# Block order, operand layout and output steps of a relative-attention kernel changed on one core

## The chip, the core and the metric

The kernel runs on one core of a Trainium2 chip. The core has TensorE (PE in the profile; PEld is its weight load), VectorE (DVE), ScalarE (ACT), GpSimd (POOL) and SyncE (SP), which here issues every transfer, and 16 DMA engines. Each engine works through its own instructions in order. The metric is the device time of one execution in microseconds (us), the median of several runs.

## What is computed

A transformer block over x of 16 sequences, 512 positions, 128 features: layer norm, then attention with relative positions (16 heads of 8 features) plus a feed-forward network (FFN) with weights of +1 and -1, plus the residual.

```python
q = (xn @ Wq + bq).reshape(B, S, H, dh)          # k, v alike; B=16, S=512, H=16, dh=8
p = (pe @ Wp).reshape(S, H, dh)
content = einsum('bihd,bjhd->bhij', q + u_bias, k)
pos = _relative_shift(einsum('bihd,jhd->bhij', q + v_bias, p))
attn = softmax((content + pos) * scale, axis=-1)
head = einsum('bhij,bjhd->bihd', attn, v).reshape(B, S, D)
out = x + head @ Wo + bo + ffn(layernorm(x))      # three layers, 256-512-512-128, relu between
```

`_relative_shift` pads one column and reshapes, so that the position score of a row comes from a window that slides with the row, and beyond the diagonal from the next row.

## The kernel before, in words

**Setup** (functions from `norm` to `more`). x is loaded by sequence (`load_x`, four buffers, XB), normalized on VectorE (`norm`, L318 to L339), transposed on TensorE (L509) and split into a high and a low half of 16 bits (`split`). FFN layers run block by block, one sequence a block (`ffn_layer`, L640, four banks of PSUM, F_BANKS; `ffn_last`, L674); ScalarE writes the high half of each result (L617), VectorE the low one (L618). The result and the residual (`ffn_residual`, added on POOL at L662) go to `res_scr` in DRAM (L691). Between these, a queue of steps of the attention's preparation is worked off at a rate set by SPAN, so that it is empty after 12.3 of 15 blocks: `project_q`, `project_k`, `project_v` per sequence, `positions` and `windows`. A projection is scaled and biased from PSUM into a 32-bit tile on ScalarE (`scaled`, L528), ScalarE casts that to its high half (`halves_to`, L502), and POOL subtracts to get the low half (L503). Content queries of two sequences are kept apart with zeros (`qu_b`, cleared at L492) and written with the zeros to `qu_scr`; keys go to `k_scr`, values in rows of 36 numbers per head to `v_scr`, position queries stay in SBUF (`qv_all`) until `quads_stored` writes them by quarter to `qv_scr`. When the queue is empty, `more` takes one step of `stores` at a time: `quads_stored(0)`, `load_head(0)`, `load_queries(0, 0)`, `quads_stored(1)`, `load_queries(0, 1)`. In setup a planner orders the instructions of each engine; it may take a ready one forward.

**Attention.** Work is cut into units. A unit is four rows of every 128-row chunk of the queries of one head, for all 16 sequences against all keys. A head has NU = 32 units in two half blocks (`up`) of UP = 16, and NL = 4 sets of position and content queries (`q_t`, two buffers, UL = 8 units to a set). Before, the order is head by head: the units of both half blocks of head 0, then head 1. `load_head` brings a head's keys, windows and values in 13 transfers, `load_queries` a set of queries in 12. They are called at the unit steps "A" and all their transfers are issued there on SP. TensorE, VectorE and ScalarE follow an order written out by hand (STEPS, one string per cycle of two units): A and B are the scores of a unit's first and second half (`scores`, L797 content, L813 and L826 position), F, G and H the maxima (L840, L845), T and N the transposes and row maxima (L850, L854), X and Y the subtraction of the maximum (L859) and the exponentials (L869), V the weighted values of the half block before (`weighted`, L887, into `a_t`). A half block of a head is called a pair in the code and takes eight V steps. During the first eight cycles, W steps do the last sequence's FFN instead of V.

**Sums.** After four V steps half the sequences of a pair are complete. `stored_sums` loads the denominators of the copied bank to `den` (L921), stores the sums by four transfers to `sum_scr`, and two V steps later `inverted` takes the reciprocals (L929), stores them (L931), and at the end of a head calls `divided`: load `raw` and `rden`, multiply on POOL (L946), store to `head_scr` (L947), all issued at once. So SP stands at L947 until POOL is done.

**Tail.** `last_steps` loads the sums of heads 0 to 14 for both half blocks (`load_sums`), the residuals (`load_res`) and the last head's denominators (`load_rden`) in the last two pairs. POOL divides the last head's first half (L978). For the last pair, `last_sums` takes the denominators by a product with `sel` (L904), reciprocals (L906) and a multiplication (L907), and `last_moved` copies to the sums. Then `output_of` multiplies all sums of both half blocks with Wo (L986), adds the residual (L994) and stores (L997).

## Time and profile before

| | |
|---|---|
| time, median of 3 runs | 1366.68 us (1365.07 to 1369.44) |
| the profiled execution | 1368.64 us |
| its span, first to last instruction | 1366.9 us, mean granted TensorE clock 0.985 |
| busy: PE, DVE, ACT, POOL | 1289.9, 1113.8, 882.3, 130.7 us |
| DMA | 243607 packets, 160.22 MB, mean 117 GB/s |
| first scores L797 / first weighted values L887 | 263.7 / 309.1 us |
| last exponentials L869 end | 1315.7 us |

The span has three stages, each read from its own rows. The setup lasts to about 264 us; FFN and preparation share the engines. From about 312 to 1312 us the written-out cycle repeats. The rest is the tail. Busy shares of the whole say little about a stage: DVE's 81% is a mean over stages with 46%, 86% and 100%. A PE row's duration contains the pipeline, so the spacing of equal matmuls is its cost: four of L640's 128x512 take 1.03 us together, one alone 0.38.

### The profile page before, as it was taken

What the parts mean: (1) busy time and instruction counts of PE and PEld (TensorE: products, weight loads), DVE (VectorE), ACT (ScalarE), POOL (GpSimd) and SP (SyncE); (2) the same over time, 40 slices, a digit from 0 to 9 for tenths busy, and PEclk for the clock granted to TensorE, in tenths of its full rate; (3) what the DMA queues carried; (4) which work ended last, traced back from release to release, by engine and by line L of the source; (5) the groups of instructions that cost most, each with busy time, mean ns of one, the idle gap of its engine ahead of it and who ended that gap; (6) DMA issues with size and microseconds to landing.
All of it is one profiled execution on the core that took longest, in us unless ns stands there. A gap on an engine that the chain in (4) does not pass through costs nothing. (4 is left out here: it accounts for less than half of the span.)

```text
span 1366.9 us, 55407 instructions
## 1 busy us (share of the span) xinstructions
PE 1289.9 (94%) x23061; PEld 952.7 (70%) x23061; DVE 1113.8 (81%) x2723; ACT 882.3 (65%) x1456; POOL 130.7 (10%) x115
## 2 busy tenths in 40 slices
PE   4988889979999999999999999999999999999966
PEld 2545555667777777777777777777777777777735
DVE  8988754678888888888888888888888888788846
ACT  4576668466666666666666666666666666666630
POOL 4243445010000000000000000000000000000011
PEclk9999999999999999999999999999999999999987
DMA  4597869863243323333333323332333353323288
GB/s 117 168 234 198 202 159 264 245 193 89 76 104 79 98 80 92 81 98 90 84 93 89 94 78 97 82 96 77 96 84 93 87 123 86 99 78 81 69 145 190
DMA packets 243607, 160.22 MB, mean 117 GB/s; under 512 B 79510, under 2 KB 227100, under 8 KB 243356
## 3 DMA queue, kind: packets, MB, share of 16 engines
q1 hardware_dynamic: 243356, 156.69, 43.9%
q8 instruction: 180, 2.95, 0.9%
q14 instruction: 71, 0.58, 0.2%
HBM read 96.34 MB, written 59.48 MB: 114 GB/s over the span
## 5 line engine op out<-in xcount | busy, mean ns | idle before, releaser
L869 ACT ACTIVATE e<-s,e_scale 128x512 f32<-128x512 f32 x1024 | 673.1, 686 | 319.9 <-PE s L859 319.5
L840 DVE TENSOR_REDUCE m<-s 128x256 bf16<-128x512 f32 x512 | 351.0, 686 | 132.0 <-PE s L826 131.9
L845 DVE TENSOR_TENSOR m<-s,m 128x256 bf16<-128x256 f32 x1024 | 428.5, 418 | 18.5 <-PE s L826 0.6
L797 PE MATMUL s<-q,k 128*128 128x64 f16 x8192 | 407.0, 193 | 4.0 <-DMA q<-qu_scr 2.1
L859 PE MATMUL s<-ident_b,nm 128*128 128x256 bf16 x2048 | 353.0, 275 | 2.3 <-DVE nm L854 2.3
L813 PE MATMUL s<-q,win 128*128 128x128 f16 (+1 forms) x4096 | 342.6, 206 | 0.0
L797 PEld LDWEIGHTS <-k 128*128 128x128 f16 x8192 | 334.3, 98 | 11.0 <-DMA q<-qu_scr 2.2
L887 PE MATMUL a_t<-e,v 128*9 128x256 f32 x4032 | 267.0, 382 | 0.7 <-ACT e L869 0.6
L813 PEld LDWEIGHTS <-win 128*128 128x128 f16 x4096 | 232.2, 98 | 0.2
L826 PE MATMUL s<-q,win_d 128*128 128x64 f16 x2048 | 227.7, 193 | 0.8 <-DMA q<-qv_scr 0.6
L859 PEld LDWEIGHTS <-nm 128*128 128x128 bf16 x2048 | 145.1, 98 | 117.2 <-DVE m L845 78.8
L854 DVE TENSOR_REDUCE nm<-t_t 128x2 bf16<-128x256 bf16 x512 | 208.8, 408 | 2.4 <-PE t_t L850 2.4
L887 PEld LDWEIGHTS a_t<-e,v 128*9 128x9 f32 x4032 | 86.5, 90 | 81.8 <-issue 2.5
L850 PE MATMUL t_t<-ident_b,m 128*128 128x128 bf16 x1024 | 141.0, 219 | 1.0 <-DVE m L845 0.9
L826 PEld LDWEIGHTS <-win_d 128*128 128x128 f16 x2048 | 130.2, 98 | 1.2 <-issue 1.1
L946 POOL TENSOR_TENSOR raw<-raw,rden 128x512 f32<-128x512 f32 x15 | 19.1, 1273 | 987.6 <-DMA rden<-rden_scr 762.8
L850 PEld LDWEIGHTS <-m 128*128 128x128 bf16 x1024 | 81.0, 97 | 32.7 <-DVE m L845 1.7
L640 PEld LDWEIGHTS <-e 128*128 128x128 f16 x512 | 49.5, 98 | 62.1 <-issue 14.8
L896 ACT COPY av<-a_t 128x256 f32<-128x256 f32 x126 | 47.0, 373 | 32.3 <-PE a_t L887 17.9
L618 DVE SCALAR_TENSOR_TENSOR h2l<-s,h2h 128x512 f16<-128x512 f32 x45 | 30.9, 686 | 37.0 <-ACT h2h L617 36.8
L640 PE MATMUL s<-h1l,e 128*128 128x512 f16 x180 | 47.1, 379 | 0.5 <-DVE h1l L618 0.4
L617 ACT ACTIVATE h2h<-s 128x512 f16<-128x512 f32 x45 | 26.9, 597 | 32.1 <-PE s L640 32.0
(176 smaller groups left out, 905.3 us busy)
## 6 DMA issues: line engine op xcount, KB each, us to landing
q<-qv_scr SPq DMA_DIRECT2D x512, 64.0 KB
q<-qu_scr SPq DMA_DIRECT2D x256, 64.0 KB
qu_scr<-k SPq DMA_DIRECT2D x32, 256.0 KB
k_scr<-hv SPq DMA_DIRECT2D x64, 128.0 KB
qu_scr<-win SPq DMA_DIRECT2D x32, 256.0 KB
qv_scr<-e SPq DMA_DIRECT2D x16, 512.0 KB
k<-k_scr SPq DMA_DIRECT2D x64, 128.0 KB
win<-p_scr SPq DMA_DIRECT2D x64, 79.5 KB
```

What stands on the lines that cost most here:

```text
L640: nc.tensor.matmul(ph, lhsT=w[:, t, f * P : (f + 1) * P], rhs=h[t][m], start=(m == 0 and t == 0), stop=(m == 1 and t == n - 1),)
L797: nc.tensor.matmul(sp[:, c % 2, :, :, 4 * g : 4 * g + 4].rearrange("p a r (n m) -> p n (a r) m", m=2), lhsT=kt[:, g, c * P : (c + 1) * P], ...
L813: nc.tensor.matmul(blocks[:, x0 : x0 + (NC + 1) * (len(cs) - 1) + 1 : NC + 1], lhsT=win[h % 2][:, side, y0 : y0 + P], rhs=qp[:, side, :, c ...
L826: nc.tensor.matmul(blocks[:, x0 : x0 + NC + 2 : NC + 1, 2 * t : 2 * t + 2], lhsT=win_d[h % 2][:, t, UP_OFF - 4 * u : WIND - 4 * u], rhs=qd ...
L840: nc.vector.tensor_reduce(st["m"], flat(st["ps"][0]).rearrange("p c x -> p x c"), AX.X, ALU.max)
L845: nc.vector.tensor_tensor(st["m"], flat(st["ps"][1])[:, c], st["m"], ALU.max)
L850: nc.tensor.transpose(st["pt"][:, f, :], st["m"][:, f * P : (f + 1) * P], ident_b)
L854: nc.vector.tensor_reduce(st["nm"], st["pt"], AX.X, ALU.max, negate=True)
L859: nc.tensor.matmul(flat(st["ps"][half])[:, :, f * P : (f + 1) * P], lhsT=st["nm"][:, f : f + 1].to_broadcast([P, P]), rhs=ident_b.unsqueez ...
L869: nc.scalar.activation(st["eT"][:, :, cs, :, i0 : i0 + 4].rearrange("p b c a r -> p (c a) b r"), st["ps"][half].rearrange("p c a r b -> p ...
L887: nc.tensor.matmul(bank[32 * r : 32 * r + VW, g], lhsT=v_t[h % 2][:, v0 : v0 + VW], rhs=pair["eT"][:, b, c], start=(c == 0 and (g == 0 or ...
L896: nc.scalar.copy(pair[half][:, g], bank[:, g])
```

## The change

The change does the following.

- **Order.** The pairs run first half block of heads 0 to 15, then the second half block of heads 0 to 15. Only two sets of queries belong to a pair; a head's keys, windows and values are loaded once for each half block. Buffers go by the pair's parity (`m`), not the head's.
- **Loads.** Scratch layouts are turned so that `load_head` is four transfers (of which the windows read overlapping runs), the values one more (`load_values`, now rows of 144 bytes from `v_scr`, stored in long runs), and `load_queries` two for content and eight for position. They are put into a list, `loading`, from which each A step issues two. Content queries come as pairs of sequences without zeros; POOL clears the half that must be zero after each load (`content`).
- **Halves.** The scale is put into the weights; `halves_to` reads the projection in PSUM twice, ScalarE for the high half, VectorE for the low one. q is projected for two sequences at once into two banks of its own. The FFN has three banks instead of four, x six buffers instead of four, SPAN is 13.4. Clearing of q_t moves from `project_k` behind `ffn_residual`; residuals are added two and two.
- **Sums.** `stored_sums` stores the whole bank in one transfer. The steps `inverted`, `inverse_stored`, `divided`, `stored` follow one another at the F steps of four cycles; `divided` works per pair (128x256) and stores straight into `all_sums` in SBUF, or for the second half block of heads 0 to 4 (EARLY) into `early_scr`, loaded later.
- **Output.** The first half block's 16 sequences are multiplied with Wo in pairs 17 to 20, each after an odd V step, in the free half of `a_t` (`first_output`; VectorE's addition, two stores and the loads of a later residual follow at an F step). The second half block's are left for the tail (`last_output`, eight steps of two sequences), where SP and ACT both issue transfers and the last two pairs' denominators are taken by `last_sums`.

```diff
+    def load_head(h, m):
+
+        k = k_scr.rearrange("t (d h) n g j -> n (t d) h (g j)", h=H)[:, :, h]
+        p = p_scr.rearrange("t (d h) s j -> (t d) h (s j)", h=H)[:, h]
+        pd = pd_scr.rearrange("t (d h) s n j -> (t d) h (s n j)", h=H)[:, h]
+        flat_p, flat_d = (t[m].rearrange("p n j -> p (n j)") for t in (win, win_d))
+        side = 2 * (WIND + 1)
+        moves = [
+            (k_t[m].rearrange("p g j -> p (g j)"), k),
+            (flat_p[:, : 2 * WIN + 4], shifted(p, 4, 1, 0, 2 * WIN + 4)),
+        ]
+        for r in range(2):
+            moves.append((flat_d[64 * r : 64 * r + 64, : side - 1], shifted(pd, 2, side, 1 - r, side - 1)))
+        return [lambda a=a: nc.sync.dma_start(*a) for a in moves]
+
+    def load_values(h, m):
+        nc.sync.dma_start(v_t[m].rearrange("p (b f) -> p b f", b=B), v_scr[:, :, h])
+
+    def load_queries(h, l):
+
+        m = l % 2
+        qv = qv_scr.rearrange("t (d h) r l a u b -> (t d) h r l (a u b)", h=H)[:, h, :, l]
+        qu = qu_scr.rearrange("t (d h) q l g i m -> (t d) h q l (g i m)", h=H)[:, h, :, l]
+
+        def content(q):
+            rows = slice(64 * q, 64 * q + 64)
+            nc.sync.dma_start(
+                qc_t[m][rows, q].rearrange("p g i m -> p (g i m)"), shifted(qu[:, q], 2, 0, 0, 8 * P)
+            )
+            for n in (2 * q, 2 * q + 1):
+                nc.gpsimd.memset(qc_t[m][32 * n : 32 * n + 32, q, :, :, 1 - n % 2], 0.0)
...
+        def halves_to(src, n, hi, lo):
+
+            nc.scalar.activation(hi, src, AF.Identity, bias=b_cols[:, n : n + 1])
+            for r in range(4) if len(src.shape) == 4 else [slice(None)]:
+                nc.vector.scalar_tensor_tensor(
+                    lo[:, r], src[:, r], b_cols[:, n : n + 1], hi[:, r], ALU.add, ALU.subtract
+                )
...
         def project_q(b):
+
+            for n in range(2):
+                nc.tensor.matmul(
+                    q_banks[:, n],
+                    lhsT=wq_d,
+                    rhs=x2T[b + n].rearrange("p (a l m) -> p l a m", a=NC, l=NL),
+                    start=True,
+                    stop=True,
+                )
+            qu = qu_b[b // 2 % 2]
+            halves_to(q_banks.rearrange("p n j -> p j n"), 0, *qu)
             for m in range(2):
                 for part in Q_PARTS[m]:
+                    nc.sync.dma_start(
+                        qu_scr[part, :, b // 2 % 2, :, b // 4], qu[m].rearrange("p (l i) n -> p l (i n)", l=NL)
+                    )
+            halves_to(
+                q_banks.rearrange("p n (q r) -> p r q n", r=4), 1, *[q[:, :, :, b : b + 2] for q in qv_all]
+            )
...
+            if 2 <= b < 10:
+                with tc.issue_after(last.ins):
+                    for n in range(2):
+                        clear_queries(2 * (b - 2) + n)
...
-        stores = [lambda: quads_stored(0), lambda: load_head(0), lambda: load_queries(0, 0)]
-        stores += [lambda: quads_stored(1), lambda: load_queries(0, 1)]
+        stores = [[lambda: quads_stored(0)], load_head(0, 0), load_queries(0, 0)]
+        stores += [[lambda: quads_stored(1)], load_queries(0, 1)]
...
+            nc.sync.dma_start(
+                sum_scr[h, :, half].rearrange("w r i -> r w i"), av.rearrange("p g i -> p (g i)")
+            )
             bs = slice(8 * half, 8 * half + 8)
-            for r in range(4):
-                b = 8 * half + 2 * r
-                dst = sum_scr[h, :, b : b + 2, up, :] if h < H - 1 else sums[up][L0:L1, b : b + 2]
-                nc.sync.dma_start(dst, av[32 * r : 32 * r + DH])
 
             def inverted():
                 nc.vector.reciprocal(den, den)
-                inv = rden_scr[h, bs, up]
-                nc.sync.dma_start(inv.rearrange("b (q m) -> b q m", q=16), den)
-                if h == H - 1:
-                    load_rden(half)
-                elif up == 1 and half == 1:
-                    divided(h)
+                return inverse_stored() if n == 2 * H - 2 else inverse_stored
+
+            def inverse_stored():
+                nc.sync.dma_start(rden_scr[h, bs].rearrange("b (q m) -> (b q) m", q=16), den)
+                if half == 1:
+                    return lambda: divided(pair, B)
+                if n == 2 * H - 2:
+                    return lambda: divided(pair, B // 2)
 
             return inverted
 
-        def divided(h):
-
-            raw, rden = (wk.tile([P, S], F32, tag=name, name=f"{name}_{h}", bufs=1) for name in ("raw", "rden"))
-            nc.sync.dma_start(raw, sum_scr[h].rearrange("w b u i -> (w b) (u i)"))
-            nc.sync.dma_start(
-                rden, rden_scr[h].rearrange("b u i -> b (u i)").unsqueeze(0).to_broadcast([DH, B, S])
-            )
+        def divided(pair, nb):
+
+            h, up = pair["h"], pair["up"]
+            raw, rden = (
+                wk.tile([P, 2 * P], F32, tag=name, name=f"{name}_{pair['n']}", bufs=1)[: DH * nb]
+                for name in ("raw", "rden")
+            )
+            nc.sync.dma_start(raw, sum_scr[h].rearrange("w x r (g i) -> w (x r g) i", g=2)[:DH, :nb])
+            nc.sync.dma_start(rden, rden_scr[h, :nb].unsqueeze(0).to_broadcast([DH, nb, 2 * P]))
             nc.gpsimd.tensor_tensor(raw, raw, rden, ALU.mult)
-            nc.sync.dma_start(head_scr[h * DH : (h + 1) * DH].rearrange("w b u i -> w b (u i)"), raw)
+            if up and h < EARLY:
+                dst = early_scr[h * DH : (h + 1) * DH]
+            else:
+                dst = all_sums[rows_of_head(h)]
+
+            def stored():
+                nc.sync.dma_start(dst[:, :nb], raw)
+
+            return stored
...
+        def first_output(b, free):
+
+            products(a_t[:, free], b)
+
+            def added():
+                t = first_res.pop(b)
+                nc.vector.tensor_tensor(t, a_t[:, free], t, ALU.add)
+                res_rows(t, 0, b, store=True)
+                load_first(b + 2)
+
+            return added
...
+        def last_output(b0, step):
+
+            out_banks.append(out_banks.pop(0))
+            po = out_banks[-1].rearrange("p (b i) -> p b i", b=2)
+            bs = slice(b0, b0 + step + 1, step)
+            for x in range(2):
+                products(po[:, x], b0 + step * x)
+            nc.vector.tensor_tensor(last_res[:, bs], po, last_res[:, bs], ALU.add)
+            for b in (b0, b0 + step) if step > 1 else (slice(b0, b0 + 2),):
+                b = b if step == 1 else slice(b, b + 1)
+                for m in range(2):
+                    (nc.sync, nc.scalar)[m].dma_start(
+                        half_rows(out, 1, m, b),
+                        last_res[64 * m : 64 * m + 64, b].rearrange("p b (k d) -> p (b k) d", d=D),
+                    )
...
+        loads = [(h, 2 * up + l) for up in range(2) for h in range(H) for l in range(2)]
...
+                if n % UL == 1 and 2 <= nl < len(loads):
+                    loading += load_queries(*loads[nl])
+                if n % UP == 1 and nl + 1 < len(loads):
+                    loading += load_head(loads[nl + 1][0], (n // UP + 1) % 2)
+                if n % UP == 4:
+                    loading.append(lambda h=h, m=n // UP % 2: load_values(h, m))
+                for _ in range(2):
+                    if loading:
+                        loading.pop(0)()
+                if n % 2 and outputs:
+                    filled.append(first_output(*outputs.pop(0)))
...
+                if n % 2 == 0:
+                    due = [more for more in (do() for do in due) if more]
...
+                if k == 0 and n == H + 1:
+                    load_first(0)
+                    load_first(1)
+                if k % 2 and H < n < H + 5:
+                    outputs.append((4 * (n - H - 1) + k // 2, k // 2 % 2 ^ 1))
+                if k == 1 and n == H + 6:
+                    nc.sync.dma_start(all_sums[: EARLY * DH], early_scr)
+                if n < 2 * H - 2:
+                    if k % 4 == 2 and later:
                         due.append(later.pop(0))
+                    if k % 4 == 3:
+                        later.append(stored_sums(pair, k // 4))
+                elif k in (2, 4):
+                    due.append(later.pop(0))
+                elif k == 3:
+                    later.append(stored_sums(pair, 0))
+                    load_last()
+                elif k == 6:
+                    last_sums(pair, 1, 0)
...
+        pair = pairs[2 * H - 1]
+        moved(pair, 0, (0, 1), [nc.sync, nc.scalar])
+        last_output(0, 1)
+        last_sums(pair, 1, 1)
+        moved(pair, 1, (0,), [nc.sync, nc.scalar])
+        last_output(2, 1)
+        moved(pair, 1, (1,), [nc.sync, nc.scalar])
+        last_output(4, 1)
+        last_output(6, 1)
+        for b in (8, 12, 9, 13):
+            last_output(b, 2)
```

## The prediction

> **What bounds the kernel now.** I read the slices of the page first, then the busy time by stage, then the order of time inside the stages in which TensorE is not full, and last the waits.
>
> ```profile
> PE   4988889979999999999999999999999999999966
> DVE  8988754678888888888888888888888888788846
> DMA  4597869863243323333333323332333353323288
> ```
>
> Three stages can be seen: a setup of eight slices (to 264 us, where the first scores start at L797), a long loop with PE at 9 everywhere, and a tail in the last two slices. The stage view gives the middle of the setup, the loop and the tail (columns: stretch, length, then busy us and count of PE, PEld, DVE, ACT, POOL, then clock, DMA share, GB/s):
>
> ```profile
> 46.00:190.00 144.00, 125.07 (x755) 74.01 (x755) 119.08 (x372) 95.81 (x170) 56.96 (x47) 0.96 0.77 204
> 312.00:1312.00 1000.00, 995.49 (x20657) 768.14 (x20655) 859.05 (x2031) 681.60 (x1107) 19.09 (x15) 1.00 0.34 89
> 1313.00:1367.00 54.00, 28.82 (x285) 20.17 (x284) 23.43 (x26) 3.70 (x9) 9.02 (x2) 0.80 0.84 170
> ```
>
> In the loop PE is the bound and DMA has two thirds free. One cycle (two units) starts every 4.03 us; the starts of L840 one after another show 7.9 us above that rhythm, half of it here, where SP issues a head's operands late:
>
> ```profile
> 1180.67 0.41 PE L797 MATMUL s<-q,k 128*128 128x64 f16 x8 [2.11 <-DMA q<-qu_scr]
> ```
>
> In the tail PE works only 29 of 54 us. The reader is to see DVE waiting in its own order for `den`, whose transfer stood behind others on SP, and all of the output product (L986) after that:
>
> ```profile
> 1331.07 0.25 DVE L929 RECIPROCAL den<-den 128x16 f32<-128x16 f32 x1 [17.55 <-DMA den<-av]
> ...
> 1336.00 4.52 POOL L978 TENSOR_TENSOR sums<-sums,e 8x2048 f32<-8x2048 f32 x1 [4.56 <-DMA e<-rden_scr]
> 1336.17 4.64 DVE L907 TENSOR_TENSOR av<-av,e 128x256 f32<-128x256 f32 x1
> ...
> 1348.48 7.31 PE L986 MATMUL s<-wo_sb,e 128*128 128x128 f32 x64
> ```
>
> L907 takes 0.43 us elsewhere; here it ends with the POOL instruction beside it. The same in setup: a VectorE instruction on SBUF operands that meets a POOL one ends when that ends (116.4 us for both below), while those that read PSUM (L618) don't stretch.
>
> ```profile
> 113.50 2.90 POOL L503 TENSOR_TENSOR e<-two,e 128x1024 f16<-128x1024 f32 x1
> ...
> 114.94 1.49 DVE L330 TENSOR_TENSOR step<-var,root 128x8 f32<-128x8 f32 x1
> ```
>
> **The change, stage by stage**, against the span of 1366.9 us.
>
> *Start (to 46 us).* PE waits 2.93 us at 17.33 behind a step of `norm` (L332) that took 3.33 us beside POOL's memsets L492 (four of 0.94 us), and 4.38 us at 34.47 behind L331, L332, L333 and L326, each 1.1 to 1.2 us beside five residual additions (L662, 1.27 us each). The memsets go; the residuals are put two and two, but the last sequence's, put far later, already ran here, so the planner may draw the others forward as well, with the clearing of q now tied behind them. Bounds -7.3 and 0; the memsets' wait goes for certain, the other I leave: **-3**.
>
> *Middle of setup (46 to 190).* Three engines count. VectorE: the low halves move to it from POOL. For two sequences q takes two of L618's 512-element instructions (0.68 each) for content and four of 256 elements (L845, 0.42) for position, 3.0 us; k takes 0.68 per sequence. For the 11 sequences of this stretch that is 24 us, 22 at the thinner rate (SPAN 12.3 to 13.4); one `norm` less gives 4 back. What POOL took from it: L335 7.8 us over its 0.34, L685 6.1 over 0.19, L330, L332, L325 and L331 11 over 0.17, together 25; POOL's 57 us fall to 8x1.27 + 16x0.53 = 19 (L662, L496), so two thirds, 17, go. Net +1: 119 becomes 120 of 144. ScalarE: L528 and L502 cost 47 us here; in their place two casts per pair at 1.15 (L502, 1024 elements) and 0.78 per k, 21. It falls from 96 to 70. PE: eight FFN blocks at 40x0.217 + 32x0.057 = 10.5 and 11 sequences at 4x0.43 + 8x0.11 + 4x0.11 = 3.0 (spacing of L640, L674, L545, L575, L509) are 117 us, so 27 us at most are to be had. Against them: FFN keeps three banks for four, so a late VectorE reaches PE sooner. With VectorE as full as before I take a quarter: **-6**, bounds -27 and +12 (half of the 25 us still lost to POOL, and PE following VectorE).
>
> *Hand-over.* Before, the chain from the first `quads_stored` (231.8) to the first scores (263.7) lies under 2.7 blocks of FFN alone (28 us). After, 1.6 blocks (17 us) are left. It needs 11.5 us for its eight stores (231.8 to 243.3, on a full DMA), 14 load issues at 0.47 (6.6) and a landing of some 4, 22 us, less what 8.4 MB fewer bytes of qu_scr save. Bounds 0 and +10: **+3**.
>
> *Loop.* The same matmuls for the heads. Removed: the waits above; sum stores are four DMAs fewer per half, operands come as 4 + 1 transfers, not 13, two per unit, and no store waits on SP for POOL behind its own load (L947 held SP 59.9 us). Of 7.9 us I take **-7** (bounds -7.9, 0). Added: the first half's output. Each of 16 sequences issues two products (four records at 0.112, from L986's 64 in 7.31), one VectorE addition of 256 (0.42), two loads and two stores on SP. PE pays 16x0.45 = **+7**; the additions hide in VectorE's 14% of idle time (6.7 us if not). `load_first` waits on SP for the store before it, and q loads stand behind it: some 2.5 us (L224 issued at 1179.10 let PE go on at 1180.67), covered by their lead. Operands of a head now come twice: 16x1.24 = 20 MB more. Per pair (32 us) 3.7 MB move; at 16.5 GB/s per engine (35.6 MB in 400 us at share 0.34) that is 0.43 of the queue. v comes in 2048 runs of 144 bytes; nearest are the out stores, 35 ns a packet, so 4.5 us of all 16 engines, 0.14 more. Share 0.6: hidden; it costs when q sets land more than their 14 us after their issue. [...] No row here has runs of 144 bytes alone. [...]
>
> POOL now clears half of each content operand after its load (four memsets of at most 0.94, L492's row) and PE waits for that. Queued ahead on POOL is the `raw` product, which waits for rden. Issue 1, landing 2.5, memsets 4: 7.5 of 14 us. Nothing.
>
> *Tail.* From 1313.0 (last V of pair 30): eight V of pair 31 at 0.9 with four `sel` products at 0.6 reach 1324; VectorE's 1.74 + 0.42 for each quarter go on beside them (third at 1325.4), no longer behind `den`. Moving the first half of head 15 to `all_sums`: two issues on each of SP and ACT at 0.6 and a landing of 2.5 from 1324.5: 1328. Then the first product and addition (0.9 + 0.7), the last quarter (0.6 + 1.74 + 0.42: 1332.3), its addition's place in VectorE's order and SP's (1333.0), four issues and a landing for the last rows: 1337; two products of 0.9, additions of 0.7: 1339.5; four issues and the landing: 1344, for 1366.9. Half of L986 (7.3 us) and of the 4 MB of out are gone from it. **-23**; bounds -27 (no wait for moves) and -15 (each of three moves 2.5 later).
>
> Sum: -3 - 6 + 3 - 7 + 7 - 23 = -29; 1366.9 - 29 = **1338 us**. The profiled execution took 1368.64 around its span, the three timed runs have a median of 1366.68, so the span stands for the median: 1338, its own range 1322 to 1352.
>
> **Rivals.**
> 1. *Operands late at the change of sets* (the slower side). There are 63 changes of q sets. Each set now passes DMA, POOL, PE, and POOL stands in order behind `raw`. For it: L797 already waits for q in the row above, and POOL waited up to 94 us for one load. Against: the DMA share of 0.34 and 14 us of lead. From 0.5 us per change it eats the 29 us; at 1 us the time is 1338 + 63 = 1401.
> 2. *VectorE sets the pace of setup.* +12 for -6 and +10 for +3, and the tail still won: 1338 + 25 = 1363. For it: VectorE is at 83% in the middle and 100% in some stretches, and gets 22 us. Against: POOL's hold on it.
> 3. *Setup reaches PE's floor*: -27 for -6: 1317. For it: ScalarE's 26 us; against: VectorE no emptier.
> 4. *The tail doesn't shorten*, DMA being the bound there (share 0.84): 1338 + 23 = 1361. Against: half of the out bytes and all of the head_scr loads leave it.
>
> **How the numbers follow.** Forecast 0.58, rival 1 0.14, rival 2 0.15, rival 3 0.09, rival 4 0.04. A difference within 0.3%, 4 us, can't be told from no change. Slower: rival 1's 0.12 and 0.02 of rival 2: 0.14. Same: 0.04 of rivals 1 and 2. Faster: 0.82. The range reaches to rival 3 and rival 2 and leaves out most of rival 1: 1312 to 1368.
>
> **What would show it.** Start of L797 near 258 (264 before); L330 to L335 without stretched durations; the loop's cycle at 4.03 us with 4.5 in 16 cycles and no waits for q; from the last V of pair 30 to the end 31 us; DMA share near 0.6 in the loop. Wrong would be: waits of PE for POOL or q at each eighth unit; DVE at 95% and PE idle before 200 us; a tail of over 40 us.

## The result, and the profile after

The changed kernel takes **1725.47 us** (median of four runs, 1719.63 to 1729.94) against 1368.06 for the kernel before, measured beside it: 1.261 times as long, interval 1.255 to 1.266. The profiled execution has a span of 1717.8 us for 1366.9. The forecast was 1338, faster.

The slices of the page after (same rows as those shown of before, and PEclk):

```profile
PE   6999985897888888888878887867578888878885
...
DVE  8998655676666666666666665555466666666664
...
PEclk9999998898898988989889898978888898898887
DMA  4655566333333333333333333323333333333343
```

Each slice of this page is 43 us, of the one before 34. The setup is fuller (9 in the second to the fifth slice, where before most read 8). But after the ninth slice PE never reads 9 again: it was 9 everywhere in the loop before. And the DMA row still reads 3, as it did before, though the operands of a head are now loaded twice. The loop needs more and gets no more.

The starts of each unit's first maxima (L840 before, L853 after) cut the span into three parts that can be held against the steps of the forecast. "Run 4" and "run 11" are experiments, told below.

| us | before | after | run 4 | run 11 | forecast, against before |
|---|---|---|---|---|---|
| start to unit 0's maxima | 265.4 | 247.9 | 247.6 | 248.7 | -3 - 6 + 3 |
| from there to unit 511's | 1045.5 | 1428.9 | 1098.4 | 1056.3 | -7 + 7 |
| from there to the end | 56.0 | 41.0 | 36.0 | 38.4 | -23 |
| span | 1366.9 | 1717.8 | 1382.0 | 1343.4 | -29 |

Start and tail lost 17.5 and 15.0 us; the loop took 383.4 more. Those come in one place: at the first and second unit of each pair. A pair lasted 32.2 to 34.3 us before (the first two aside, in which the last sequence is finished) and lasts 38.9 to 48.3 now, and 51 to 56 in pairs 18 to 21, where the first outputs are made. Here is such a place, from the timeline (start, us, engine, line; in brackets the idle time before, and what ended it):

```profile
522.36 0.55 SPq L205 DMA_DIRECT2D k<-k_scr  x1
...
523.80 0.54 SPq L205 DMA_DIRECT2D win<-p_scr  x1
524.38 3.23 SPq L205 DMA_DIRECT2D win_d<-pd_scr  x2
...
527.72 3.12 SPq L208 DMA_DIRECT2D v<-v_scr  x1
530.89 6.29 SPq L968 DMA_DIRECT2D raw<-sum_scr  x1
537.28 1.02 SPq L218 DMA_DIRECT2D q<-qu_scr  x2
...
543.15 1.35 POOL L222 MEMSET q<- 32x512 f16 x2 [21.14 <-DMA q<-qu_scr]
545.73 1.35 POOL L222 MEMSET q<- 32x512 f16 x2 [1.22 <-DMA q<-qu_scr]
...
547.13 0.59 PE L810 MATMUL s<-q,k 128*128 128x64 f16 x8 [5.53 <-POOL q L222]
```

SP issues a transfer in some 0.5 us; here it is held 3.2 us by the two `win_d`, 3.1 by `v` and 6.3 by `raw`. So the next set's content, two pieces (L218), is issued at 537.28 only, lands at 543 and 546, POOL clears it, and PE goes on at 547. The stage view of the same moments says why (length, then busy us and count of PE, PEld, DVE, ACT, POOL, then clock, DMA share, GB/s):

```profile
520.00:525.00 5.00, 5.00 (x110) 4.05 (x109) 4.02 (x10) 3.60 (x7) 1.35 (x2) 1.00 0.36 98
525.00:530.00 5.00, 5.00 (x120) 4.08 (x117) 4.53 (x12) 3.56 (x6) 0.00 (x0) 1.00 0.26 95
530.00:535.00 5.00, 5.00 (x107) 3.86 (x107) 4.40 (x11) 2.91 (x5) 0.00 (x0) 1.00 0.59 134
535.00:540.00 5.00, 5.00 (x102) 3.44 (x102) 4.40 (x12) 3.85 (x7) 0.00 (x0) 1.00 0.31 73
540.00:545.00 5.00, 1.60 (x38) 1.43 (x34) 2.19 (x5) 1.38 (x3) 1.31 (x2) 1.00 0.36 104
```

`k`, `win`, `win_d` and `v`, issued from 522 to 531, are 1.3 MB, so from 525 to 530 there is enough to move; SP is held, and the DMA share is 0.26. Four of sixteen engines are 0.25. The share is low because the transfers don't use more, not because there is nothing to move. Over the whole execution the waits are for the same loads of `q`, the content (`qu_scr`) and the position queries (`qv_scr`) (engine, line, what it waited for; total us, times, longest):

```profile
POOL q L222 <- DMA q<-qu_scr: 1040.7, 122, 49.7
...
PE s L810 <- POOL q L222: 167.6, 30, 13.1
...
PE s L826 <- DMA q<-qv_scr: 99.3, 36, 5.6
```

That is 167.6 and 99.3 us of PE's time, with waits of PEld beside them. Rival 1 of the prediction had this place, POOL's clearing behind late content.

### The profile page after: what moved, and what is told of

Same layout as the page of the kernel before. It is cut to its first block, busy times and chain, and to the rows that moved or that the text cites. A ratio compares the mean times of both kernels' runs of the same rounds, so it can differ in the third digit from the quotient of the medians.

```text
span 1717.8 us, 55528 instructions
## 1 busy us (share of the span) xinstructions
PE 1383.1 (81%) x23065; PEld 1005.7 (59%) x23065; DVE 1131.2 (66%) x2793; ACT 853.5 (50%) x1399; POOL 229.8 (13%) x340
## 4 chain that ended last, share of the span: by engine, by line
PE 53%; DMA 31%; DVE 7%; SPq 6%; issue 2%; ACT 1%; POOL 0%; POOLq 0%; DVEq 0%; ACTq 0%
DMA q<-qu_scr 15%; PE a_t L899 11%; PE s L872 11%; PE s L810 10%; DMA q<-qv_scr 10%; PE s L826 8%; DMA out_dram<-o 4%; PE p L635 4%; PE s L839 3%; PE t_t L863 3%; SPq L218 1%; SPq L230 1%; SPq L990 1%; SPq L968 1%; DVE h2l L613 1%
## 5 line engine op out<-in xcount | busy, mean ns | idle before, releaser
L853 DVE TENSOR_REDUCE m<-s 128x256 bf16<-128x512 f32 x512 | 351.7, 687 | 453.9 <-PE s L839 442.2
L810 PE MATMUL s<-q,k 128*128 128x64 f16 x8192 | 423.9, 197 | 177.0 <-POOL q L222 167.6
L810 PEld LDWEIGHTS <-k 128*128 128x128 f16 x8192 | 352.3, 101 | 186.9 <-DMA q<-qv_scr 106.5
L826 PE MATMUL s<-q,win 128*128 128x128 f16 (+1 forms) x4096 | 355.9, 212 | 99.7 <-DMA q<-qv_scr 99.3
L872 PE MATMUL s<-ident_b,nm 128*128 128x256 bf16 x2048 | 373.7, 288 | 13.4 <-DVE nm L867 13.4
L222 POOL MEMSET q<- 32x512 f16 x256 | 170.3, 665 | 1085.1 <-DMA q<-qu_scr 1040.7
L826 PEld LDWEIGHTS <-win 128*128 128x128 f16 x4096 | 242.5, 101 | 104.6 <-DMA q<-qv_scr 77.9
L899 PE MATMUL a_t<-e,v 128*9 128x256 f32 x4032 | 291.6, 411 | 0.0
L635 PE MATMUL p<-h1l,e 128*128 128x512 f16 x240 | 62.9, 382 | 0.0
L635 PE MATMUL p<-h1h,e 128*128 128x512 f16 x240 | 62.2, 379 | 0.0
L612 ACT ACTIVATE h2h<-p 128x512 f16<-128x512 f32 x60 | 35.8, 597 | 47.5 <-PE p L635 44.2
```

The source lines that it names most:

```text
L222: nc.gpsimd.memset(qc_t[m][32 * n : 32 * n + 32, q, :, :, 1 - n % 2], 0.0)
L635: nc.tensor.matmul(ph, lhsT=w[:, t, f * P : (f + 1) * P], rhs=h[t][m], start=(m == 0 and t == 0), stop=(m == 1 and t == n - 1),)
L810: nc.tensor.matmul(sp[:, c % 2, :, :, 4 * g : 4 * g + 4].rearrange("p a r (n m) -> p n (a r) m", m=2), lhsT=kt[:, g, c * P : (c + 1) * P], ...
L826: nc.tensor.matmul(blocks[:, x0 : x0 + (NC + 1) * (len(cs) - 1) + 1 : NC + 1], lhsT=win[side_m][:, side, y0 : y0 + P], rhs=qp[:, side, :, ...
L853: nc.vector.tensor_reduce(st["max"], flat(st["ps"][0]).rearrange("p c x -> p x c"), AX.X, ALU.max)
L872: nc.tensor.matmul(flat(st["ps"][half])[:, :, f * P : (f + 1) * P], lhsT=st["nm"][:, f : f + 1].to_broadcast([P, P]), rhs=ident_b.unsqueez ...
```

## The experiments

The theory to be tested, A in the expectations: the new transfers are written with an outermost dimension of 4 (`k`, `win`, the sums) or 2 (`win_d`, content), and each runs on just that many of the 16 DMA engines, always the same ones. The share of 0.26 above agrees with the count for `k`.

The records of the single packets in the trace show how many are under way at once. From 300 to 880 us it is exactly four for 68.8 of the 94.2 us in which `k`'s packets (4096 bytes) move, and never more than six; four for 33.0 of 63.0 us of `win`'s (2552 bytes); two for 27.8 of 47.9 us of the two `win_d`'s (1010 bytes). Content and sums both have packets of 2048 bytes: two for 137.7 of 270.6 us, four for 62.4. The stores to `v_scr`, written with 128 outermost (2304 bytes, 46 to 190 us), have 16 under way longer than any other count, 3.8 of 14.6 us.

The 128 packets of `k` in the pair shown move from 523.7 to 531.2, four or five at a time for 4.7 us of it. Those of `win`, issued 1.4 us behind `k`, move only from 529.7, as `k` runs out, to 534.8, and those of `win_d` until 536.9. From 525 to 531 never more than seven packets of any kind are under way at once. So these transfers stand behind one another. That they do so on the same engines is an inference, for the records don't say which of the 16 a packet uses; the sums speak for it. Their store is issued at 540.45, behind content. Of the 256 packets of the two, 192 start before 545.3; the last 64, half of the sums, move two at a time from 545.7 to 548.5, after the last content has landed (POOL goes on at 545.73), as if they had stood behind it on its two engines. `raw`'s issue, which holds SP, ends at 537.2, when `win_d` has moved. In pairs 3 to 16 `k`'s packets take 6.3 to 8.2 us in this kernel and 2.3 to 3.8 in run 4 below, where up to 18 are recorded at once.

Runs 1 to 4 move the same bytes to the same places, but in pieces of 32 rows. "Before" was 1368.22 beside them.

**Run 1, content alone in pieces of 32 rows.**

```diff
-            nc.sync.dma_start(
-                qc_t[m][rows, q].rearrange("p g i m -> p (g i m)"), shifted(qu[:, q], 2, 0, 0, 8 * P)
-            )
+            for n in (2 * q, 2 * q + 1):
+                nc.sync.dma_start(
+                    qc_t[m][32 * n : 32 * n + 32, q].rearrange("p g i m -> p (g i m)"), qu[:, q]
+                )
```

> The two content transfers of a set (64 rows, leading dimension 2 in the source) become four of 32 rows; bytes and order stay. Theory A (transfers whose outermost dimension is 2 or 4 run on only 2 or 4 of the 16 DMA engines, always the same ones, which are then full for longer than a pair's 32 us): the two fullest engines lose some 11 of 38 us per pair; time 1420 to 1560. Theory B (the 144-byte rows of the values fill the queue and hold SP): no change, 1700 to 1740. Theory C (PE waits for POOL, which clears half of the content and stands in order behind the product of raw and rden): no change beyond 2%, 1690 to 1750.

Measured: 1621.69 us, ratio 1.185 (1.179 to 1.190). The direction is the theory's, the size less than it said: 104 of the 357 us over the kernel before. SP is still held in this run, 3.4 us by `v` (mean of pairs 3 to 17) and 6.6 by the first content piece behind it (pair 5), so content still goes out late, whatever its own form.

**Run 2, a head's keys and windows alone in pieces of 32 rows** (L205).

```diff
+        q4 = [slice(32 * n, 32 * n + 32) for n in range(4)]
+        size = 2 * WIN + 4
         moves = [
-            (k_t[m].rearrange("p g j -> p (g j)"), k),
-            (flat_p[:, : 2 * WIN + 4], shifted(p, 4, 1, 0, 2 * WIN + 4)),
+            [(k_t[m][q4[n]].rearrange("p g j -> p (g j)"), k[n]) for n in range(4)],
+            [(flat_p[q4[n], :size], p[:, n : n + size]) for n in range(4)],
         ]
...
```

> Keys, windows and diagonal windows go in pieces of 32 rows (12 transfers for 4), issued at the same four steps. Theory A: the 8 us in which keys move at a DMA share of 0.26 shrink to 2, SP is no longer held while it issues, the next content goes out in time: 1400 to 1560, the larger part of the loss if SP's being held counts more than the engines' load. Theory B: the values still hold SP at the load of raw (6.3 us): above 1650. Theory C: 1690 to 1750.

Measured: 1521.93, ratio 1.112 (1.109 to 1.115): the largest single part, 204 of the 357 us. SP now issues `v` in 0.57 us and `raw` in 0.43 (means of pairs 3 to 17; 3.23 and 6.63 in the changed kernel), though the edit touches neither: what held SP at them was the transfers ahead of them.

**Run 3, the store of the sums alone in four.**

```diff
-            nc.sync.dma_start(
-                sum_scr[h, :, half].rearrange("w r i -> r w i"), av.rearrange("p g i -> p (g i)")
-            )
+            for r in range(4):
+                nc.sync.dma_start(
+                    sum_scr[h, :, half, r], av[32 * r : 32 * r + 32].rearrange("p g i -> p (g i)")
+                )
```

> The store of the sums goes in four pieces of 32 rows. Theory A: the four fullest engines lose 5 of 38 us per pair: 1580 to 1690. Theories B and C: no change, 1690 to 1750.

Measured: 1693.81, ratio 1.237: 32 us, a little less than the theory's least.

**Run 4, the three together.**

> All three splits together: no operand transfer with an outermost dimension of 2 or 4 is left in the loop. Theory A: the stalls at the start of each pair (some 10 us each, 332 us in all) go nearly all: 1360 to 1430, with the stalls of pairs 18 to 21 (some 45 us, where SP waits for a store of out before it loads a residual) left. Theory B: above 1550. Theory C: 1690 to 1750.

Measured: 1383.27, ratio 1.011 (1.008 to 1.013). So 342 of the 357 us come from the form of three kinds of transfer; bytes, order, POOL's clearing and the doubled loads are all still there. The three alone gave 104, 204 and 32, 339 in sum. The stage view of runs after and 4, over the same stretch of the loop (all before the first outputs):

```profile
312.00:880.00 568.00, 471.29 (x9080) 357.08 (x9072) 380.76 (x891) 299.38 (x486) 77.98 (x116) 0.90 0.33 91
```

```profile
312.00:880.00 568.00, 562.10 (x11652) 435.51 (x11650) 485.66 (x1146) 383.13 (x623) 104.97 (x156) 1.00 0.46 119
```

The reader is to see that the share goes *up*, 0.33 to 0.46, when the kernel gets faster. The clock reads 0.90 in the changed kernel, where PE is busy for 471.3 of the 568 us, and 1.00 in run 4, where it is for 562.1.

What is left in run 4 lies in pairs 18 to 24, 47 us over the rhythm. There SP issues nearly without a pause. From the rows of SP's timeline, pair 5 (plain loop) and pair 20 (transfers issued, us of the rows, which hold short gaps between issues too, length of the pair):

| | plain pair | pair 20 |
|---|---|---|
| before | 42, 20.6 of 32.3 | (no first outputs) |
| after | 34, 29.9 of 42.8 | 50, 34.2 of 56.4 |
| run 4 | 52, 26.7 of 32.3 | 68, 38.9 of 43.5 |
| run 5 | 44, 22.7 of 32.5 | 60, 34.9 of 39.4 |
| run 11 | 44, 25.4 of 32.5 | 50, 27.7 of 33.3 |

After has the fewest transfers of all and yet its SP is busy longest in a plain pair: 0.88 us for each transfer, 0.51 in run 4. And in run 4 pair 20 has 38.9 us of issue where the rhythm is 32.2. Runs 5, 6, 8 and 10 test whether SP's issue sets what is left ("before" 1369.7).

**Run 5, keys and sums laid out in DRAM so that one transfer of 128 rows does what four did.**

```diff
-    k_scr = scr("k_scr", [4, DH * H, 4, 4, S], F16)
+    k_scr = scr("k_scr", [4, 4, DH * H, 4, S], F16)
-    sum_scr = scr("sum_scr", [H, 32, 2, 4, 4 * P], F32)
+    sum_scr = scr("sum_scr", [H, 2, 4, 32, 4 * P], F32)
-        k = k_scr.rearrange("t (d h) n g j -> n (t d) h (g j)", h=H)[:, :, h]
+        k = k_scr.rearrange("n t (d h) g j -> (n t d) h (g j)", h=H)[:, h]
...
-                sum_scr[h, :, half].rearrange("w r i -> r w i"), av.rearrange("p g i -> p (g i)")
+                sum_scr[h, half].rearrange("r w i -> (r w) i"), av.rearrange("p g i -> p (g i)")
...
```

> All three kinds of transfer in pieces as in the fourth run, but keys and sums laid out in DRAM so that one transfer of 128 rows does what four of 32 did: 3 + 6 issues on SP fewer per pair and one more (raw in two). Theory S, that in pairs 18 to 24 SP has more transfers to issue than a pair is long (some 68 at 0.45 to 0.65 us): 8 fewer are 4 to 5 us in each of the four worst pairs (43 to 44 us now) and something in their neighbours, 15 to 30 us in all: 1353 to 1368. Rival D, that the DMA engines' load or the wait of the first outputs' loads for their stores sets these stalls: within 5 us of the fourth run, 1378 to 1388.

Measured: 1360.41, ratio 0.993 (0.991 to 0.995): theory S, and 0.7% less than the kernel before. Here a single transfer with an outermost dimension of 128, one quarter of the issues, was no worse than four. That it moves "by 16 engines", as the expectations of runs 8 and 9 say, fits the 16 packets of the stores to `v_scr` above; for keys and sums of this run no count is given here, so there it is an estimate.

**Run 6, run 4 with the first outputs' transfers issued by ScalarE** (`nc.sync` to `nc.scalar` in `res_rows`).

> The fourth run with the first outputs' loads and stores issued by ScalarE instead of SP: some 16 transfers, 10 us of issue, leave SP in each of pairs 17 to 20. Theory S (SP's issue sets the stalls there): those pairs come to 33 to 36 us, 30 to 45 us less in all: 1338 to 1353. Rival D (DMA load, or the loads' wait for their stores): pairs stay at 42 to 44, 1378 to 1390. Rival E, that ScalarE, busy 22 of 32 us in the loop, can't take 10 us of issue and the waits with it: pairs of 36 to 44 and ScalarE the releaser, 1360 to 1390.

Measured: 1407.53, ratio 1.028 (1.023 to 1.033), slower than run 4 and above all three ranges; of the mechanisms, rival E's. Pairs 18 to 21 take 49.6, 48.2, 49.3, 43.6. ScalarE's timeline:

```profile
868.56 1.29 ACTq L1001 DMA_DIRECT2D out_dram<-o  x2
872.78 1.29 ACTq L999 DMA_DIRECT2D o<-res_scr  x2
874.11 2.42 ACT L890 ACTIVATE e<-s,e_scale 128x512 f32<-128x512 f32 x4 [5.25 <-DMA win_d<-pd_scr]
```

The load stands in ScalarE's order before the exponentials. The profile puts their wait down to a transfer of `win_d`, which none of them reads; what lies between 869.9 and 874.1 on ScalarE is the load, issued 2.9 us after the store whose buffer it takes. ScalarE, busy some 22 us of a pair (681.6 us in the 1000 us of the loop before), has slack in the sum, and here none for a wait in the middle of its order: the exponentials stood 5.25 us.

**Run 8, runs 5 and 6 together.**

> The fifth and sixth runs together: keys and sums by 16 engines in one transfer each, first outputs issued by ScalarE. Theory S: no pair over 36 us, 1335 to 1350, faster than the kernel before. Rival D: 1375 to 1390. Rival E: 1355 to 1385.

Measured: 1399.04, ratio 1.021 (1.018 to 1.025): rival E's mechanism again, above its range. Pairs 18 to 21: 45.2, 50.0, 50.7, 46.2.

**Run 9, run 5 with the last half block's sums in a place of their own.** In the tail ScalarE's copy into the `av` buffer waited for the moves out of it:

```profile
1334.51 4.09 SPq L940 DMA_DIRECT2D sums<-av  x6
1338.70 0.37 ACT L916 COPY av<-a_t 128x256 f32<-128x256 f32 x1 [8.51 <-DMA sums<-av]
```

```diff
+            if g == 0 and c == 0 and at_end and half:
+                pair[half] = v_t[1 - pair["m"]][:, : 4 * P].rearrange("p (g i) -> p g i", g=2)
...
```

> The fifth run (keys and sums by 16 engines) with the sums of the last half block put in a place of their own (the values of the pair before, which are dead) instead of the buffer that the moves of pair 30 still read. In the fifth run ScalarE's copy L916 waited 8.51 us for those moves at 1338.70 and TensorE stood from 1333.3 to 1339.1. Theory T, that this wait sets the tail: 4 to 6 us less, 1354 to 1357. Rival, that the chain through SP's moves ends as late without it: 1359 to 1362.

Measured: 1357.58 ("before" 1365.47 for runs 9 to 12), ratio 0.994 (0.992 to 0.996): between the two ranges, and against the kernel before no less than run 5's 0.993, so the time shows no gain. In the traces the part behind unit 511's maxima goes from 40.1 to 37.8, 2 us and not 4 to 6: the next thing was nearly as late. In run 9 PE waits for the same six issues of SP, now by way of the output product:

```profile
1332.55 4.15 SPq L942 DMA_DIRECT2D sums<-av  x6
1337.61 2.05 PE L1017 MATMUL s<-wo_sb,sums 128*128 128x128 f32 x8 [5.70 <-DMA sums<-av]
```

**Run 10, run 5 with the first outputs spread over eight pairs.**

```diff
-EARLY = 5
+EARLY = 9
-                if k % 2 and H < n < H + 5:
-                    outputs.append((4 * (n - H - 1) + k // 2, k // 2 % 2 ^ 1))
-                if k == 1 and n == H + 6:
+                if k % 4 == 1 and H < n < H + 9:
+                    outputs.append((2 * (n - H - 1) + k // 4, 1))
+                if k == 1 and n == H + 10:
```

> The fifth run with the 16 first outputs spread over eight pairs, two in each, instead of four pairs with four. Theory S (SP's issue is over its time only while first outputs run, 60 issues in a pair of 32 us at 0.45 to 0.65): 52 issues fit or nearly so, pairs 18 to 25 come to 33 to 35 us in place of four of 40: 8 to 20 us less, 1340 to 1353. Rival R, that each issue over a limit costs its time wherever it stands: eight pairs of 36, the same sum, 1356 to 1364.

Measured: 1344.15, ratio 0.984 (0.980 to 0.987): theory S. Spreading also leaves each load of a residual longer after the store whose buffer it takes, so this run alone doesn't exclude that wait; run 5, where only the issues of keys and sums became fewer, had already gained more than that rival allows. Pairs 18 to 25 take 33.3 us each, 1.05 over the rhythm. PE is busy for all of their 266.4 us, so this is the work of two outputs, 0.53 each, and no wait is left.

**Run 11, the edits of runs 9 and 10 together.**

> The ninth and tenth runs' edits together on the fifth. If theories S and T hold: 1336 to 1348, 1.4 to 2.3% faster than the kernel before. If neither does: 1357 to 1363.

Measured: 1341.40 (1338.25 to 1345.18, five runs), ratio 0.982 (0.979 to 0.984), 1.9% faster than the kernel before, with the change's order of half blocks, its halves from PSUM and its doubled loads all in it. Its difference from run 10 lies within the intervals of both. Its slices, to be held against the two pages shown:

```profile
PE   6889999889999999999999999999999999999996
...
DMA  4555457773344444444444444444454444544453
```

The other runs ask what made the **setup** 17 us shorter, which the prediction put down to POOL's hold on VectorE. **Run 7** put idle POOL work behind each low half.

> The fourth run with idle two-input POOL work of 128x512 put behind each low half in setup (two behind each q step, one behind each k step), about as much POOL time as the kernel before had for its low halves. Theory P, that the setup became 17 us shorter because POOL no longer holds VectorE's SBUF instructions: the first maxima start at 256 to 266 (247.6 in the fourth run) and the time is 1391 to 1402. Rival Q, that it is ScalarE's relief (two of its passes over each projection gone): the start moves by less than 4 us, 1381 to 1388.

Measured: 1420.08, ratio 1.037, maxima from 270.5: above the theory's range. But the work wasn't where it was meant to be. Nothing depended on it, and POOL ran it all at once:

```profile
12.34 23.50 POOL L531 TENSOR_TENSOR idle<-idle 128x512 f32<-128x512 f32 x21
...
46.48 11.19 POOL L531 TENSOR_TENSOR idle<-idle 128x512 f32<-128x512 f32 x10
```

The run shows that POOL held for 50 us early in the setup costs some 23; it says nothing of the middle. **Run 12** ties the idle work to the low halves by reading them (`nc.gpsimd.tensor_tensor(idle, lo2, hi2, ALU.subtract)`).

> The fourth run with idle POOL subtractions that read the low halves just made (three of 1024 elements behind each content step of two sequences, one of 1024 strided over two passes of 512 behind each k), so that they can't be drawn ahead as those of the seventh run were (48 of 50 us of them lay before 77 us). About 45 us of POOL work between 46 and 200 us, what the kernel before had more than this one. Theory P, that POOL's hold on VectorE was worth the 17 us by which setup became shorter: first maxima at 257 to 268 (247.6 in the fourth run), 1392 to 1404. Rival Q, ScalarE's relief: start moves by less than 4 us, 1381 to 1388.

Measured: 1391.60, ratio 1.018 (1.015 to 1.021). The middle of the setup, run 4 and then run 12:

```profile
46.00:190.00 144.00, 136.95 (x879) 80.49 (x878) 127.33 (x411) 84.93 (x146) 16.17 (x19) 1.00 0.57 174
```

```profile
46.00:190.00 144.00, 133.29 (x840) 76.90 (x839) 129.41 (x407) 82.85 (x143) 49.26 (x48) 1.00 0.56 171
```

POOL works 33 us more in this stretch, PE 3.7 less, and the first maxima come at 250.7 for 247.6. The stand-in is a fair one in this respect: VectorE's L356 takes 499 ns a piece here, as its L335 did in the kernel before, and 338 in run 4. It gives 3 us of 17, and that is no more than the spread of kernels with one and the same setup code: runs 5 and 8 to 11 start between 244.6 and 249.8, the changed kernel at 247.9 and run 3 at 252.6. The time as a whole falls between the ranges of both theories. **Run 13** gives ScalarE idle casts (`nc.scalar.copy(idle, hv[0])`, four for each k), and **run 14** sets SPAN and the buffers of x back to 12.3 and four ("before" 1365.98).

> The fourth run with four idle ScalarE casts of 128x512 behind the cast of each k in setup, 2.5 us per sequence: what ScalarE has less to do per sequence than in the kernel before (4.3 us of L528 and L502 there, 1.8 us of L522 here). Theory Q, that ScalarE's relief shortened the setup: first maxima at 257 to 268 (247.6 in the fourth run), 1392 to 1404. Rival N, that it is neither POOL nor ScalarE but the rate and the buffers that the change also set: 245 to 251, 1380 to 1388.

> The fourth run with SPAN back at 12.3 and four buffers of x in place of six, as in the kernel before. Theory N (rate and buffers made the setup shorter): first maxima at 256 to 266, 1391 to 1402. Theory Q (ScalarE's relief): 245 to 252, 1380 to 1389.

Measured: 1381.32 (maxima from 242.8) and 1384.42 (from 245.6). Neither moves the start later, though in run 13 ScalarE works 110.8 us from 46 to 190, more than the kernel before (95.8; run 4 84.9). **Run 15** has the idle work of 12 and 13 together.

> The idle POOL subtractions of the twelfth run and the idle ScalarE casts of the thirteenth together, on the fourth run. If the two removed loads act together (each hidden behind the other when put back alone): first maxima at 256 to 268, 1391 to 1406. If they add up as they did alone (3 us and none): 247 to 253, 1382 to 1392, and neither is what shortened the setup.

Measured: 1400.58, with two times 15 us apart; its profiled execution has a span of 1391.2 and starts its maxima at 250.9, as run 12. So POOL and ScalarE together carry some 3 us, no more than the spread, and the rate and buffers none that can be seen. What carries the other 14 stays open. Not tried by themselves were the load on DMA, whose share from 46 to 190 fell from 0.77 to 0.57 (run 4), q projected for two sequences at once, the three banks, and the order of instructions that the planner makes.

## Why the prediction was wrong, point by point

**The step that failed** is the doubled operands: "At 16.5 GB/s per engine ... that is 0.43 of the queue ... Share 0.6: hidden". It treats the 16 engines as one pool, into which 3.7 MB per pair fall. The figure was a mean over the loop before, whose operands came in pieces of 32 rows. Of the new transfers, `k` at 512 KB, moving at the 95 GB/s of the row 525 to 530, takes 5.5 us at a share of a quarter. An estimate for the engines that carry the most, if they are always the same, from that rate (24 GB/s an engine), from the counts of packets and from the sizes in the profile: `k` 5.5, `win` 319 KB on four 3.4, two `win_d` of 63 KB on two 2.7, four content pieces of 128 KB on two 10.9, two sums of 256 KB on four 5.5, together 28 us of a 32 us pair, and a part of all else on top, while the other twelve carry only their part of that. The mean share of 0.34 in the loop, which was the argument "against" rival 1, can't show this. Nor was the forecast's mean too low: it said 0.6, the changed kernel has 0.33, and run 4, with the same bytes, 0.46.

**Removed issues on SP** were counted as a gain ("operands come as 4 + 1 transfers, not 13"). SP issued 34 a pair for 42, but was held for 0.88 us each instead of 0.49. `k` itself is issued in 0.55 us; SP is held at what comes behind it, most at `raw`, and run 2, with keys and windows in pieces, no longer has that.

**Rival 1** had the place (change of sets; DMA, POOL, PE one after another) and the wrong cause (POOL in order behind `raw`) with too small a price: 1 us at each of 63 changes. It measured some 10.5 us at each change of the head, 31 of them, and next to nothing at the changes inside a pair until the first outputs came. POOL's clearing, costed at nothing, does cost nothing once the transfers are right: in run 10 the plain pairs from the third on run at 32.2 to 32.6 but for one of 33.9, and in run 11 PE waits for POOL's q once, 0.9 us.

**First outputs, +7.** PE's part measured 8.4, 16 at 0.53 for 0.45. The transfers did not: "`load_first` waits on SP for the store before it, and q loads stand behind it ... covered by their lead". That reckons with single waits, not with SP's sum: 68 issues take 38.9 us in a pair of 32. It costs some 39 of run 4's 47 us (8.4 are the products) and is gone in runs 10 and 11, where a pair has 50 to 52.

**The loop's old waits, -7.** About half of them went. Over a rhythm of 32.25, pairs 2 to 30 held 8.1 us before and 12.1 in run 11, of which 8.4 are the products: some 3.6 are left, so -4.5. The two ends of the loop, for which the sum has no term, cost 6.8: the first two pairs take 74.6 us for 71.6, the last one 34.3 for 30.5 up to its last maxima. (With the rate and the buffers of before, in run 14, the first two take 70.1, for 74.0 in run 4.) So the loop of run 11 is 10.7 us longer than before where 0 was forecast.

**Start, -3.** The first 46 us hold 29.4 us of PE's work for 26.7: -2.8. The number is right, but by luck: of the two waits named, 2.9 and 4.4 us, only 0.8 us is left, and a new one of 3.7 us, for `wp_d` from VectorE at 41.25, takes half of it back.

**Middle, -6, and hand-over, +3.** PE's idle time from 46 to 190 went from 18.9 us to 3.4 (after) and 7.0 (run 4): -12 to -16, in the range (-27 to +12), but the taken value was too timid. The stated reason, VectorE freed of POOL, is worth 3 us of it at most by run 12, and most of it has no shown cause. The hand-over brought no loss in run 4, where PE works 54.6 of the 55 us from 190 to 245; in the changed kernel it works 50.1.

**Tail, -23.** -15.0 after, -20.0 in run 4, -17.6 in run 11. The mechanism was right. Missing was SP's order: six moves are issued in one go of 4.1 us and PE waits for them, which the estimate had as two issues on each of two queues.

With the pieces right, the outputs spread and a buffer freed, run 11 stands at -23.5 in its span, 5.5 us from the sum of -29. That is closer than its terms were: the setup gave -16.6 for -6, the loop +10.7 for 0, the tail -17.6 for -23, and these errors partly cancel. Of the changed kernel's 357 us over the one before, 342 come from one property of a transfer that can be read off the code and that no mean shows. The 144-byte runs of v were not tried by themselves; in run 11 nothing waits for v, and the records of its 2048 packets in a pair add up to 29 us, 1.8 us of all 16 engines where the prediction took 4.5.

## What to carry to other kernels

Read the outermost dimension of every new transfer, on both of its sides (`k` had the 4 in its source, the sums in their destination), and where it is as small as here (4 or 2) cost the transfer on that many engines: with it `k` moved four packets at a time and took 6.3 to 8.2 us, in four pieces 2.3 to 3.8 (run 4). A low DMA share over a stretch in which an issuer is held isn't room: it was 0.26 here while SP was held for 3.2 us at `win_d` and 3.1 at `v`. And sum SP's issues per period, at some 0.5 us each (0.51 in run 4): 38.9 us of them went with a pair of 43.5 where the rhythm is 32.2, and spreading them in time (run 10, 1344.15 us) did better here than moving them to ScalarE's queue (run 8, 1399.04).

## What the runs showed of the hardware that was not expected

- At a share of 0.26, with four or five packets under way, 95 GB/s were moved: on four engines 24 GB/s each, an estimate, where the loop before made 16.5 of its own share.
- The transfers with two or four packets under way held SP at what came behind them: 3.2 us at `v` and 6.6 at `raw` on average, 0.57 and 0.43 when keys and windows were in pieces (run 2). `k` itself took 0.55 us to issue in one piece, and 2.0 in four (run 4).
- 33 us more of two-input work on POOL in the setup's middle cost PE 3.7 us there, though it stretches single VectorE instructions: L356 took 499 ns a piece (run 12) for 338 without it (run 4).
